# Moving layer 0's sums of h from GpSimd in the setup to VectorE in the first scores

## The chip, the cores and the metric
One core of a Trainium2 chip runs the whole program. Its engines are TensorE (PE, with its weight loads PEld), VectorE (DVE), ScalarE (ACT), GpSimd (POOL) and SyncE (SP, which here only issues DMAs). The metric is the time of one execution on the device in microseconds, the median of several runs.

## The reference
Two graph layers over N = 2708 nodes with D = 1024 features; `adj` is a sparse matrix of zeros and ones.
```python
# layer 0
h = jnp.maximum(_layernorm(x), 0.0)
f = h @ Wf + bf;  g = h @ Wg + bg
e = relu(f @ g.T)
attention = softmax(where(adj > 0, e, NEG), axis=1)
x = x + attention @ (h @ W + bW)
# layer 1
h = jnp.maximum(_layernorm(x), 0.0)
h1 = h @ W1
e = leaky_relu((h1 @ a1) + (h1 @ a2).T, 0.2)
x = x + relu(softmax(where(adj > 0, e, NEG), axis=1) @ h1)
```
All arithmetic is in float32.

## The kernel before, in words
**Panels and pairs.** The 2708 rows of the result are done in five panels of 512 to 576 columns (NP = 5). The contracted nodes lie in 20 full tiles of 128 rows, joined to ten pairs (NQ = 10), and two small tiles (MONO and TINY, together the unit LEFT).

**Seven products for eight.** Every large matrix product is done as a two-by-two block product with seven products, M1 to M7, in place of eight (a Strassen-Winograd scheme). It needs sums and differences of the blocks beforehand. For the product attention @ h the left blocks are rows of h: of a pair, ha = (ha0, ha1) and hb = (hb0, hb1), each half 128x512. The products use ha0 (M1), hb0 (M2), hb1 (M4), and four sums: s1 = ha1 + hb1 (M5), s2 = s1 - ha0 (M6), s3 = ha0 - ha1 (M7) and s4 = hb0 - s2 (M3). They are kept in device memory in `hg_d`, seven planes for each group of two pairs, and `aggregate` (from line 788) loads them as `hc`.

**Order of layer 0.** First a setup: the product M of the two weight matrices (`half_row_of_M`, from line 479), with the preparation of h in between. `make_pairs` (from line 336) puts the pieces of that preparation in a list `later`: for each pair, load x (`fetch`), layer norm (`normalize`: moments on VectorE, square root and scaling on ScalarE), `rows` (calls `pair_h`, line 297: the four sums above and the stores of the seven planes), `transposes` (TensorE, copied by ScalarE to the tiles hsT), dots with the vector vb (VectorE, lines 215 to 221, the result goes to `junk`), and `last` (line 373: sums of the transposed blocks on VectorE, stores to `hs_d`). Then `project_q(0)` (line 590) makes the right factor B of the first panel, and `scores(0)` (line 1055) multiplies the transposed rows, loaded as `As` from `hs_d` (line 1074), by B. For each pair q it also loads adjacency squares for q + 2 (`adj_i`, `adj_t`), turns them to masks, and has VectorE add the partial products. Then comes `project_q(1)`, with the softmax of panel 0 in between, then `aggregate(0, 0, ...)`, then the other panels and layer 1.

**What sets the order of the work.** A piece in `later` has a cost written by hand in microseconds. `behind(us)` (line 197) is called after groups of matmuls; it adds `us` to a credit, of at most twice `us`, and runs pieces while the credit is above zero. In `scores` the rate is 1.3 while pairs are still to be made, afterwards, for panel 0, 0.6; there are seven such units for a pair. `one()` (line 188) first issues the loads of the first `ahead[0]` pieces of the list, then runs the first piece. `ahead[0]` is 5 at the start and becomes 2 after `scores(0)` (line 1363).

**Queues and buffers.** All `load`s (line 137) go out on SP in program order; a load whose buffer isn't free holds up all that follow it. `store`s (line 141) go out on GpSimd's queue. Two sets of buffers matter: `slots`, 54 of 128x576, and `stream`, 12 of 128x1024. x, the score tiles, B, masks and scratch are slots; hsT, As, adj_i, hc, md and the tiles g1 and g2 of `pair_h` (two sums each, line 317) are streams. In `scores` VectorE's instructions keep their program order (`nc.hold`).

In layer 0 `pair_h` uses GpSimd (line 300) and always takes the way through g1 and g2, lines 317 to 327. In layer 1 it uses VectorE.

Of the kernel before, what the change touches and what calls it, by code (L numbers as in the profile page):

```python
# [19 lines left out]
W = 512  # L20
# [5 lines left out]
M1, M5, M6, M7, M3, M2, M4 = range(7)  # L26
# [31 lines left out]
def kernel(  # L58
# [230 lines left out]
    def left_h(l, hm, ht):  # L289

        for e in range(2):
            store(hgl_d[l][:, e, :W], hm[e])
            for d in range(NH):
                g = slice(B32 * d, B32 * (d + 1))
                store(hgl_d[l][g, e, W:], ht[e][g, d * P:(d + 1) * P])

    def pair_h(l, q, ha, hb):

        n = P
        on = nc.vector if l else nc.gpsimd  # L300
        if l and q >= NQ - F // 2:
            s1, s2, s3, s4 = (slot(f"g{i}")[:, :W] for i in range(4))
            i, j = group_of[q]
            for m, h in ((M1, ha[0]), (M2, hb[0]), (M4, hb[1])):
                store(hg_d[l][i][:n, m, j], h)
            on.tensor_tensor(s1, ha[1], hb[1], OP.add)
            on.tensor_tensor(s2, s1, ha[0], OP.subtract)
            for m, h in ((M5, s1), (M6, s2)):
                store(hg_d[l][i][:n, m, j], h)

            def rest():
                on.tensor_tensor(s4, hb[0], s2, OP.subtract)
                on.tensor_tensor(s3, ha[0], ha[1], OP.subtract)
                for m, h in ((M3, s4), (M7, s3)):
                    store(hg_d[l][i][:n, m, j], h)
            return rest
        g1, g2 = stream("g1", (P, 2, W)), stream("g2", (P, 2, W))
        s1, s2, s3, s4 = g1[:n, 0], g1[:n, 1], g2[:n, 0], g2[:n, 1]
        on.tensor_tensor(s1, ha[1], hb[1], OP.add)
        on.tensor_tensor(s2, s1, ha[0], OP.subtract)  # L320
        on.tensor_tensor(s3, ha[0], ha[1], OP.subtract)
        on.tensor_tensor(s4, hb[0], s2, OP.subtract)
        i, j = group_of[q]
        for m, h in ((M1, ha[0]), (M2, hb[0]), (M4, hb[1])):
            store(hg_d[l][i][:n, m, j], h)
        store(hg_d[l][i][:n, M5:M6 + 1, j], g1[:n])
        store(hg_d[l][i][:n, M7:M3 + 1, j], g2[:n])

    u = consts.tile([P, NC], FP, name="u")
    v = consts.tile([P, NC], FP, name="v")  # L330
    c0 = consts.tile([P, 1], FP, name="c0")
# [4 lines left out]
    def make_pairs():  # L336
        xs, hT = {}, {}

        def fetch(q):
            xs[q] = []  # L340
            for t in units[q]:
                xs[q].append(row_halves("x"))
                load_rows_of(t, xs[q][-1], x)

        def rows(q):
            left_h(0, *xs[q]) if q == LEFT else pair_h(0, q, *xs[q])

        def turned(q, k, e):
            t = units[q][k]
            ps = bank("h_ps", (P, NH, P))  # L350
            for c in range(NH):
                nc.tensor.transpose(ps[:, c, :], xs[q][k][e][:, c * P:(c + 1) * P], ident)
            for i, (s, n) in enumerate(pieces[0]):
                if s == t:
                    o = first_h[e].rearrange("p (c i) -> p c i", c=NH)[:, :, i * P:i * P + n]
                    nc.vector.tensor_copy(o, ps[:, :, :n])
            return ps

        def transposes(q):
            if q == LEFT:  # L360
                two = stream("hsl", (P, 2, NH, P))
                for e in range(2):
                    nc.scalar.copy(two[:, e], turned(q, 0, e))
                    nc.scalar.copy(tinyT[:, e], turned(q, 1, e)[:, :, :B32])
                store(hsl_d.rearrange("p e c j -> p (e c j)"), two.rearrange("p e c j -> p (e c j)"))
            else:
                ts = [stream("hsT", (P, 2, NH, P)) for _ in range(4)]
                hT[q] = ts, lambda i: ts[i // 2][:, i % 2]
                for k, e, i in ((0, 0, 0), (0, 1, 3), (1, 0, 7), (1, 1, 6)):
                    nc.scalar.copy(hT[q][1](i), turned(q, k, e))  # L370
            turned_tiles.update(units[q])

        def sums(q):
            if q == LEFT:
                return
            ts, i = hT.pop(q)
            at = {m: i(k) for k, m in enumerate(BY_SCORES)}
            add(at[M5], i(7), at[M4])
            sub(at[M6], at[M5], at[M1])
            sub(at[M7], at[M1], i(7))  # L380
            sub(at[M3], at[M2], at[M6])
            for g, t in enumerate(ts):
                store(hs_d[q][:, 2 * g:2 * g + 2].rearrange("p m c j -> p (m c j)"), t.rearrange("p m c j -> p (m c j)"))

        def dots(q, k):
            t = units[q][k]
            c = col_of[t]
            dot(r_[:, c:c + 1], xs[q][k], [vb[e][:, :W] for e in range(2)], c0)
            if t == MONO:
                nc.gpsimd.dma_start(r_[:NM, HALF:HALF + 1], r_[NM:, c:c + 1])  # L390

        def drop(q, what):
            seen.setdefault(q, set()).add(what)
            if len(seen[q]) == 3:
                xs.pop(q)

        def last(q):
            sums(q)
            drop(q, "sums")
            made.add(q)  # L400

        def bias(q, k):
            dots(q, k)
            drop(q, f"dots{k}")

        seen = {}
        def put_norms(q):
            put(2.1, lambda: normalize(xs[q][0]), lambda: fetch(q))
            put(2.1, lambda: normalize(xs[q][1]))

        put_rows = lambda q: put(0.5, lambda: rows(q))
        def put_dots(q):
            for k in range(2):
                put(1.6, lambda k=k: bias(q, k), ready=lambda: vb[0] is not None)

        todo = [0, 1, LEFT] + list(range(2, NQ))
        put_norms(todo[0])
        for i, q in enumerate(todo):
            if i + 1 < len(todo):
                put_norms(todo[i + 1])  # L420
            put_rows(q)
            put(0.5, lambda q=q: transposes(q), takes_psum=True)
            if i > 1:
                put_dots(q)
            put(2.7 if q != LEFT else 0.0, lambda q=q: last(q))
            if i == 1:
                put_dots(todo[0])
                put_dots(todo[1])

    def make_until(q):  # L430
        while min(q, NQ - 1) not in made:
# [342 lines left out]

    exps, LAG = [0], 2

    def exps_until(n):
        while exps[0] < n:
            one()
# [275 lines left out]
    def scores(p, B):  # L1055
# [46 lines left out]
        for q in range(NQ):  # L1102
            n = P
            make_until(q + 2)
            rate = 1.3 if NQ - 1 not in made else rates[p]
            if q + 2 <= LEFT:
                fetch(q + 2)
            sa, sb = slot("Sa"), slot("Sb")
            S[pairs[q][0]], S[pairs[q][1]] = sa, sb
            X, Y, Z = (bank(f"s{k}") for k in "xyz")  # L1110
            m1, t = slot("sm1"), slot("st")
            product(q, M1, X, True)
            for s in (lo, hi):
                add(m1[:n, s], X[:n, :h], rb[:n, s])
            if left_over:
                left_over()
            product(q, M6, Z, True)
            add(t[:n, lo], Z[:n, :h], m1[:n, hi])
            behind(rate, True)
            product(q, M5, Y, True)  # L1120
            add(t[:n, hi], Y[:n, :h], m1[:n, hi])
            if q + 1 <= LEFT:
                convert(q + 1)
            behind(rate, True)
            product(q, M2, X, False)
            add(sa[:n, lo], X[:n, :h], rb[:n, lo])
            if q + 1 <= LEFT:
                turn(q + 1, 0)
            behind(rate, True)
            product(q, M7, Z, False)  # L1130
            add(sb[:n, hi], Z[:n, :h], t[:n, hi])
            if q + 1 <= LEFT:
                turn(q + 1, 1)
            behind(rate, True)
            product(q, M3, Y, False)
            add(sa[:n, hi], Y[:n, :h], t[:n, lo])
            finish(q, sa, 0)
            behind(2 * rate, True)
            left_over = lambda q=q, sb=sb, Z=Z, m1=m1: last(q, sb, Z, m1)
# [220 lines left out]
    for p in range(NP):  # L1360
# [7 lines left out]
        else:  # L1368
# [2 lines left out]
            nc.hold = ()  # L1371
            scores_before()
        then = {M5: prepare_W} if p == 0 else {}
        if p == NP - 2:
            then[M2] = lambda: first_masks(NP - 1, 0)
            then[M6] = lambda: first_masks(NP - 1, 1)
            then[M7] = lambda: first_masks(NP - 1, 2)
# [132 lines left out]
```

## Time and profile before
| | |
|---|---|
| median of 4 runs | 3138.29 us (3137.76 to 3142.21) |
| the profiled execution | 3142.21 us, of which the span of the profile is 3140.1 us |
| DMA | 651.82 MB, mean 208 GB/s |
| setup | 0 to 152 us; `project_q(0)` 152 to 233; `scores(0)` 233 to 401 |
| GpSimd's sums in layer 0 (lines 319 to 322) | 40, each about 1.3 us, from 71 to 276 us |

How to read it: the page gives busy time, share of the span and count of instructions for each engine. A line of a timeline has start, duration (both us), engine, line, operation, out<-in and count. A line of waits has who waited, for whom, us in total, how often, and the longest. Almost all VectorE and ScalarE instructions show line 45, since a helper records them; they are told apart by their tiles. A table by stage lists, for each stretch, its length, busy us (and counts) of PE, PEld, DVE, ACT and POOL, then the granted clock of TensorE, the mean busy share of the 16 DMA engines, and GB/s.

### The profile page before, as it was taken

How to read it: one execution, taken by the hardware profiler on the slowest of the kernel's cores; microseconds unless marked ns; L12 is line 12 of the kernel's file. 1: busy time of each engine (PE TensorE's matmuls, PEld its weight loads, DVE VectorE, ACT ScalarE, POOL GpSimd, SP SyncE). 2: the span in 40 equal slices, each digit the busy share in tenths (PEclk: the TensorE clock that was granted, in tenths of full speed). 3: DMA queues.
4: the chain of work that ended last, by engine and by line, in shares of the span. 5: the costliest groups of instructions: out<-in, count | busy, mean ns of one | idle time of the engine just before them, and what ended most of it. 6: DMA issues, size and time to landing. Idle time of an engine off the chain costs nothing.

```text
span 3140.1 us, 36230 instructions
## 1 busy us (share of the span) xinstructions
PE 3052.8 (97%) x12712; PEld 2265.0 (72%) x12712; DVE 1826.9 (58%) x3730; ACT 447.2 (14%) x788; POOL 465.4 (15%) x668
## 2 busy tenths in 40 slices
PE   8988999999999999999999999998999999999998
PEld 4566777767877588876888885865757758678684
DVE  5867686286732687427872478659473571745612
ACT  3321020000200101000020002103031130311200
POOL 2643002210002110023000101021010020120202
PEclk9989999999999999999999999998999999999999
DMA  6889837878446796468955678596555565565655
GB/s 211 311 280 277 260 125 301 227 236 242 157 133 161 221 251 213 145 157 254 290 174 151 170 217 246 190 294 243 192 182 170 158 200 159 167 197 171 216 162 190
DMA packets 379109, 651.82 MB, mean 208 GB/s; under 512 B 170848, under 2 KB 211328, under 8 KB 378928
## 3 DMA queue, kind: packets, MB, share of 16 engines
q1 hardware_dynamic: 335920, 525.38, 54.6%
q0 software_dynamic: 43008, 124.13, 11.8%
q8 instruction: 101, 1.65, 0.2%
q14 instruction: 80, 0.66, 0.1%
HBM read 536.68 MB, written 112.67 MB: 207 GB/s over the span
## 4 chain that ended last, share of the span: by engine, by line
PE 85%; DMA 5%; DVE 4%; issue 3%; POOL 1%; SPq 1%; ACT 0%; POOLq 0%; DVEq 0%; ACTq 0%
PE gy L567 12%; PE gz L567 12%; PE gx L567 11%; PE sz L1077 7%; PE gv L567 5%; PE pz L969 5%; PE sx L1077 5%; PE sy L1077 4%; PE px L969 4%; PE py L969 4%; PE qz L567 3%; PE qy L567 2%; PE qx L567 2%; PE M_ps L483 2%; DMA maskl<-mk_d 1%
## 5 line engine op out<-in xcount | busy, mean ns | idle before, releaser
L1077 PE MATMUL sz<-B,As 128*128 128x288 f32 (+2 forms) x1200 | 293.0, 393 | 8.2 <-DVE st L45 7.5
L1077 PEld LDWEIGHTS sz<-B,As 128*128 128x128 f32 x1200 | 227.8, 191 | 58.4 <-DVE st L45 11.9
L873 POOL TENSOR_TENSOR gT<-gT,rr 128x2304 f32<-128x2304 f32 (+5 forms) x20 | 72.7, 3637 | 1102.9 <-DVE rr L45 1000.0
L1077 PE MATMUL sx<-B,As 128*128 128x288 f32 (+2 forms) x800 | 201.5, 395 | 13.0 <-DMA As<-hs_d 12.2
L1077 PE MATMUL sy<-B,As 128*128 128x288 f32 (+2 forms) x800 | 199.0, 392 | 0.0
L567 PE MATMUL gz<-P,hc 128*128 128x288 f32 (+2 forms) x800 | 186.0, 393 | 2.3 <-ACT gT L45 2.3
L567 PE MATMUL gz<-Sa,hc 128*128 128x288 f32 (+2 forms) x800 | 186.0, 393 | 2.3 <-ACT gT L45 2.3
L567 PE MATMUL gx<-P,hc 128*128 128x288 f32 (+2 forms) x800 | 186.8, 395 | 0.1
L1077 PEld LDWEIGHTS sx<-B,As 128*128 128x128 f32 x800 | 152.4, 191 | 44.8 <-DMA As<-hs_d 12.7
L567 PE MATMUL gy<-T,hc 128*128 128x288 f32 (+2 forms) x800 | 184.2, 391 | 0.0
L567 PEld LDWEIGHTS gx<-P,hc 128*128 128x128 f32 x800 | 153.5, 192 | 33.2 <-issue 1.9
L567 PEld LDWEIGHTS gz<-Sa,hc 128*128 128x128 f32 x800 | 151.2, 190 | 36.0 <-ACT gT L45 4.4
L567 PEld LDWEIGHTS gz<-P,hc 128*128 128x128 f32 x800 | 150.9, 190 | 35.7 <-ACT gT L45 4.5
L567 PEld LDWEIGHTS gy<-T,hc 128*128 128x128 f32 x800 | 152.0, 190 | 30.5
L1077 PEld LDWEIGHTS sy<-B,As 128*128 128x128 f32 x800 | 151.7, 190 | 30.6 <-DVE st L45 0.3
L969 PE MATMUL pz<-w,ps 128*128 128x512 f32 x320 | 142.1, 594 | 0.8 <-DVE pt L45 0.8
L969 PE MATMUL py<-w,ps 128*128 128x512 f32 x320 | 142.2, 593 | 0.0
L969 PE MATMUL px<-w,gT 128*128 128x512 f32 x320 | 141.8, 595 | 0.0
L143 POOL DMA_DIRECT2D out_dram<-x_res x180 | 89.2, 502 | 265.0 <-DVE x_res L45 242.3
L45 DVE TENSOR_TENSOR gT<-gy,u 128x288 f32<-128x288 f32 (+2 forms) x40 | 14.8, 431 | 183.5 <-PE gy L832 183.5
L45 DVE TENSOR_TENSOR u<-gz,m 128x288 f32<-128x288 f32 (+2 forms) x40 | 17.6, 439 | 171.2 <-PE gz L567 170.8
L143 POOL DMA_DIRECT2D mk_d<-mask x55 | 36.0, 655 | 543.2 <-DVE mask L45 520.0
(318 smaller groups left out, 5093.3 us busy)
## 6 DMA issues: line engine op xcount, KB each, us to landing
hc<-hg_d SPq DMA_DIRECT2D x350, 512.0 KB, 3.9
As<-hs_d SPq DMA_DIRECT2D x150, 512.0 KB, 5.2
w<-wt_d SPq DMA_DIRECT2D x96, 512.0 KB, 5.3
w<-in_L_gnn_W_dram SPq DMA_DIRECT2D x72, 512.0 KB, 4.2
md<-md_d SPq DMA_DIRECT2D x56, 512.0 KB, 4.5
adj_i<-in_adj_dram SPq DMA_DIRECT2D x200, 128.0 KB, 4.9
hs_d<-hsT POOLq DMA_DIRECT2D x40, 512.0 KB, 5.0
hg_d<-g POOLq DMA_DIRECT2D x36, 512.0 KB, 4.9
```

The costliest lines, as they stand in the source:

```text
L45: i = f(*a, **k)
L143: nc.gpsimd.dma_start(a, b)
L483: nc.tensor.matmul(ps, wfT[a][c // NH][:, c % NH, :], wgT[b][c], start=(c == 0), stop=(c == NC - 1))
L567: nc.tensor.matmul(ps[d], left(m, k, d), right(m, k), start=(start and k == 0), stop=(k == K - 1 and m not in more), skip_group_check=True)
L873: nc.gpsimd.tensor_tensor(of(e, s), of(e, s), by(s, k), OP.mult)
L969: nc.tensor.matmul(ps, left[i][m][:, k, :], w_[k], start=(start and k == 0), stop=(k == NH - 1), skip_group_check=True)
L1077: nc.tensor.matmul(ps[:n, :h], lefts[q][:, i % 2, c, :n], B[m][c // 2][:, c % 2, :h], start=(start and c == 0), stop=(c == NH - 1), skip_g ...
```

## The change
In layer 0 `rows` no longer calls `pair_h`. It stores ha0, ha1, hb0 and hb1 as they are, ha1 for now in the plane of M5. When all pieces of the preparation have been put in the list, `sums_h` puts two more pieces for each pair: the first has the four rows read back into four slots `hr` and makes s1 and s3 on VectorE in place, the second makes s2 and s4 and stores the four sums to their planes. Each has a written cost of 1.4. In `scores`, once all pairs are made, `ahead[0]` becomes 2. The first aggregation, after M1, runs whatever of these pieces is left.
```diff
     def pair_h(l, q, ha, hb):
...
-        on = nc.vector if l else nc.gpsimd
-        if l and q >= NQ - F // 2:
+        on = nc.vector
+        if q >= NQ - F // 2:
...
+    def rows_h(q, ha, hb):
+        i, j = group_of[q]
+        for m, h in ((M1, ha[0]), (M5, ha[1]), (M2, hb[0]), (M4, hb[1])):
+            store(hg_d[0][i][:, m, j], h)
+
+    summed = [0]
+
+    def sums_h():
+        def fetch(q, two):
+            i, j = group_of[q]
+            for m in (M1, M5, M2, M4):
+                two.append(slot("hr")[:, :W])
+                load(two[-1], hg_d[0][i][:, m, j])
+
+        def first(q, two):
+            a0, a1, b0, b1 = two
+            add(b1, a1, b1)
+            sub(a1, a0, a1)
+
+        def second(q, two):
+            a0, a1, b0, b1 = two
+            sub(a0, b1, a0)
+            sub(b0, b0, a0)
+            i, j = group_of[q]
+            for m, t in ((M5, b1), (M6, a0), (M7, a1), (M3, b0)):
+                store(hg_d[0][i][:, m, j], t)
+            summed[0] += 1
+        for q in range(NQ):
+            two = []
+            put(1.4, lambda q=q, two=two: first(q, two), lambda q=q, two=two: fetch(q, two))
+            put(1.4, lambda q=q, two=two: second(q, two))
...
-            left_h(0, *xs[q]) if q == LEFT else pair_h(0, q, *xs[q])
+            left_h(0, *xs[q]) if q == LEFT else rows_h(q, *xs[q])
...
+        sums_h()
...
+    def sums_until_all():
+        while summed[0] < NQ:
+            one()
...
             rate = 1.3 if NQ - 1 not in made else rates[p]
+            if NQ - 1 in made:
+                ahead[0] = 2
...
+        if p == 0:
+            then[M1] = sums_until_all
```

## The prediction
> **What bounds the kernel now.** I read the shares of the page first, then the windows of the first 609 us, then what TensorE waits for in them, then the timelines of the engines named there. The page says that TensorE is the bound of the whole:
> ```profile
> PE 3052.8 (97%) x12712; PEld 2265.0 (72%) x12712; DVE 1826.9 (58%) x3730; ACT 447.2 (14%) x788; POOL 465.4 (15%) x668
> ```
> So a change that adds no TensorE work can win only where TensorE stands still: 3140.1 - 3052.8 = 87 us in all. The table by stage (busy us of each engine, clock, DMA share, GB/s) shows how much of that lies in the part that is changed:
> ```profile
> 100.00:186.00 86.00, 71.39 (x229) 40.19 (x227) 74.73 (x143) 32.23 (x63) 58.94 (x85) 0.92 0.92 323
> 186.00:231.00 45.00, 44.61 (x181) 34.94 (x182) 23.95 (x53) 9.39 (x19) 19.15 (x24) 0.93 0.72 245
> 231.00:279.00 48.00, 35.19 (x156) 27.28 (x155) 34.73 (x81) 9.52 (x18) 21.51 (x27) 0.88 0.84 279
> 279.00:388.00 109.00, 109.00 (x456) 85.54 (x455) 72.53 (x155) 2.05 (x4) 5.99 (x11) 0.99 0.94 271
> ```
> Second number: TensorE; fourth: VectorE; sixth: GpSimd. In 100 to 186 TensorE is idle 14.6 us, VectorE nearly full, GpSimd busy 59. In 231 to 279 it is idle 12.8. In 279 to 388, the rest of the first scores, it never stops, but DMA is busy 0.94. The waits of TensorE name the three holes:
> ```profile
> PE sx L1077 <- DMA As<-hs_d: 12.2, 1, 12.2
> PE qx L567 <- ACT m L45: 8.9, 1, 8.9
> PE h_ps L352 <- ACT M L45: 5.2, 1, 5.2
> ```
> **Holes two and three are VectorE's, and it is GpSimd that holds it up.** ScalarE copies in order behind a square root that waits for VectorE's moments. The two timelines, side by side in time:
> ```profile
> 153.57 4.41 DVE L45 SCALAR_TENSOR_TENSOR junk<-x,vb 128x512 bf16<-128x512 f32 x1
> ...
> 158.52 0.74 DVE L45 SCALAR_TENSOR_TENSOR r<-part,c 128x1 f32<-128x1 f32 x1
> ```
> ```profile
> 153.71 1.28 POOL L319 TENSOR_TENSOR g<-x 128x512 f32<-128x512 f32 x1
> 154.95 1.26 POOL L321 TENSOR_TENSOR g<-x 128x512 f32<-128x512 f32 x1
> 156.17 1.25 POOL L320 TENSOR_TENSOR g<-g,x 128x512 f32<-128x512 f32 x1
> ```
> The same VectorE instruction takes 0.69 us elsewhere; here it ends only when three GpSimd sums have ended.
>
> **Hole one is a queue.** SP stands at adj_i from 252.3 until a stream buffer comes free, and the rows As of the third pair are behind it. What frees the buffer is the store of GpSimd's sums, as the chain of waits and SP's timeline show:
> ```profile
> 259.70 3.23 DMA hg_d<-g
> ```
> ```profile
> 262.98 3.71 SPq L139 DMA_DIRECT2D adj_i<-in_adj_dram  x4
> 266.74 2.57 SPq L139 DMA_DIRECT2D adj_t<-in_adj_dram  x4
> 269.41 9.70 SPq L139 DMA_DIRECT2D As<-hs_d  x4
> ```
> **What the Trainium skill says.** "SBUF — State Buffer", section Who interferes with whom: a VectorE instruction with two SBUF inputs contends with a GpSimd instruction that reads SBUF, and the loser is blocked for the whole instruction. The trace agrees, and more: 4.41 us spans three of them. "GPSIMD Engine Reference", section Elementwise: a two-input add is about twice as slow there as on VectorE. Here 1.27 us against 0.68 us (hsT sums of the same size), 1.9 times. "DMA: Bandwidth & Descriptors", section Issuing engines are not separate DMA queues: what SP and GpSimd issue runs on the same 16 DMA engines. That matters below; 0.82 of q1 and 0.12 of q0 add up to the 0.94 of 279 to 388.
>
> **The change, part by part.**
>
> (a) *Removed: 40 GpSimd sums* in the setup, 52.7 us of GpSimd (12.8 + 12.7 + 13.6 + 13.6). GpSimd is not the bound; the worth is what VectorE gets back. Excess over the normal duration of the same form, from 100 to 186: 110.4 us 1.2; 112.8 0.4; 115.1 1.2; 125.3 1.2; 135.4 3.7; 153.6 3.7; 158.5 0.5; 173.3 (hT, 4.48 against 1.35) 3.1; 177.9 0.9. Sum 16 us, against 14.6 us of TensorE idle. VectorE's 74.7 busy us become 59; with its hand-overs to ScalarE (the idle 11 us) that is 70 against TensorE's 71. So the two holes nearly close, and the ScalarE hand-overs (0.4 to 0.9 us each) become the late ones. I take 12 us; bounds 6 (the loads of x, whose buffers come late, end the waits instead) and 14.6 (all of it).
>
> (b) *Removed: two stream buffers a pair* (g1, g2) and three 256 KB stores a pair in the setup (7 become 4). For hole one the next buffer to come free is that of the hsT sums before, whose stores are issued by 249.3 us and land some 5 us later, at 254 instead of 263. From there, as now: 6.4 us to the As load, 5.6 us landing: 266, and TensorE, ready at 262.9, waits 3 us, not 12. I take 9; bounds 5 and 12.8.
>
> (c) *Added to VectorE: 40 sums* of 0.68 us, 27 us, in the first scores. By the queue's credit, seven steps of 0.6 a pair allow three pieces of 1.4 a pair, so they begin at the end of the third pair and are done in the ninth, six sums or 4.1 us a pair. VectorE is idle 109 - 72.5 = 36.5 us there; 8.7 of 13.6 us a pair becomes 12.8. Behind a late sum stand, in VectorE's written order, the adds that empty the accumulators; TensorE rewrites one two products (3.9 us) after it filled it, so a lag of about 3 us is free. I take 0; bounds 0 and 3. GpSimd's 40 new issues of 0.55 us lie in its idle time: 0. The first aggregation's check for unfinished sums finds none: 0.
>
> (d) *Added: 40 loads on SP and 40 stores on GpSimd's queue*, 256 KB each, 21.0 MB, nearly all from 279 to 388. There 29.6 MB move now. Of these 4.7 MB (nine md loads for the next stage) and of the new some 1.5 MB (last stores) can land later: 29.6 + 21.0 - 4.7 - 1.5 = 44.4 MB in 109 us, 407 GB/s. The highest long rate in the trace is 412 (500 to 525 us, large packets); with adj's packets under 512 B among them the busiest four-microsecond stretches give 375 to 380. At 380 the bytes take 117 us, 8 us too many. I take 8; bounds 0 (412 GB/s holds) and 25 (331 GB/s, the most that any of these stages reaches in 14 us, gives 134).
>
> (e) *SP's order.* Three pairs of rows (12 loads) are fetched in the third pair already, ahead of the adj and As loads of the fourth. At 0.47 us an issue (As: 1.90 us for four) that is 5.7 us; those As loads are now issued 8 us ahead of use and land in 5 to 7, so about 3 us are exposed. I take 3; bounds 0 and 8. From the fourth pair on SP's lead over TensorE is 10 to 17 us.
>
> The shorter look-ahead (2 for 5) takes hold only once all pairs are made and touches nothing but these sums. Nothing after the first aggregation changes: 0.
>
> **The sum.** -12 - 9 + 0 + 8 + 3 = -10 us. The profiled execution took 3142.21 us (span 3140.1), so it becomes 3132; the median of the four runs lies 3.9 lower, so **3128 us**. About 0.2% (6.3 us) is what a measurement of this kernel can tell from no change.
>
> **The rivals.**
>
> *Given back in the scores (22%).* The 21 us are won, but (d) costs 18 (44.4 MB at 350 GB/s take 127 us) and (e) 3: as before, 3138. For it: DMA at 0.94 already. Against it: share above 1 occurs[...], so the share overstates how full the engines are.
>
> *SP blocked by single buffers (27%): slower.* The rows read back take four slots a pair, and by the eighth pair some 43 of 54 slots are taken (18 score tiles, 14 of B, masks and scratch). A load of rows that waits on SP for the store of the sums two pieces before stands ahead of eight adj loads (4.5 us) and the As load (5 to 7 us landing). Once SP's lead is gone TensorE waits about 6 us a pair; over six pairs 36. 36 + 3 - 21 = 18 slower: 3156. It decides from a wait of SP longer than the 10 us lead, and needs four pairs of waits to end slower than before. For it: hole one is just such a wait. Against it: slots are short only from the seventh pair on, where it would cost 12 (then 3133, my forecast still).
>
> *Only the wins (14%).* (d) and (e) hidden by an earlier start of the loads: 3138 - 20 = 3118.
>
> *The change not doing what it says* can be excluded: all four sums of layer 0 have VectorE as engine.
>
> **How the numbers follow.** Forecast 37%, only wins 14%, given back 22%, blocked 27%. Forecast and only wins give 51% faster. Of given back, 21 fall within 0.2% and 1 beyond it on the slow side; with blocked that makes 28% slower. The faster cases' own range is 3115 to 3134. For 8 in 10 I reach from 3114 (27 won, of 14.6 + 12.8, less 3) to 3154, which holds most of the blocked case.
>
> **What would show it.** (a) right: the dot with vb stays at 0.69 us everywhere, ScalarE's wait for moments shrinks, TensorE's idle time in the setup falls below 5 us. (b) right: the 12.2 us wait for As is under 5. (d) or (e): TensorE waits for As in the pairs from the fourth on, with DMA near 400 GB/s. Blocked: SP waits on stores of the sums. Wrong altogether if the two holes stay with GpSimd silent: then x loads, not VectorE, bound the setup.

## The result, and the profile after
| | before | after |
|---|---|---|
| median | 3139.17 us (3135.99 to 3143.37, 61 runs) | 3144.10 us (3141.27 to 3148.44, 41 runs) |
| the profiled execution | 3142.21 us, span 3140.1 | 3142.71 us, span 3140.9 |
| ratio after / before | | 1.0016, 95% interval 1.0012 to 1.0021 |

The change makes the kernel 5 us slower; 10 us faster had been forecast. The two profiled executions lie at opposite ends of their kernels' spread (the one before 3.0 us above its median, the one after 1.4 below), so their spans differ by only 0.8 us. The traces can show where about 15 us were won and as many lost; they cannot place the last 4 of the 5.

TensorE's work is what it was (3052.8 us busy before), and so is its share:
```profile
PE 3052.6 (97%) x12712; PEld 2264.7 (72%) x12712; DVE 1825.4 (58%) x3770; ACT 447.7 (14%) x788; POOL 426.1 (14%) x658
```
What differs is where it stands still. First the table by stage of the kernel after (second number TensorE, fourth VectorE, sixth GpSimd, then clock, DMA share and GB/s), in the same stretches as before; the kernel is about 15 us further on from 186 us:
```profile
100.00:186.00 86.00, 86.00 (x305) 52.30 (x304) 60.67 (x146) 34.63 (x66) 31.84 (x59) 1.00 0.92 319
186.00:231.00 45.00, 45.00 (x206) 35.79 (x206) 33.26 (x75) 8.13 (x17) 7.54 (x14) 1.00 0.69 228
231.00:279.00 48.00, 33.73 (x141) 25.61 (x140) 32.03 (x75) 7.32 (x13) 8.64 (x16) 0.89 1.01 327
279.00:388.00 109.00, 94.73 (x367) 72.27 (x366) 79.52 (x155) 0.00 (x0) 23.84 (x44) 0.94 1.02 338
```
Three readings. In 100 to 186 TensorE now never stops: 14.6 us won. In 231 to 279 it is idle 48 - 33.7 = 14.3 us, where it was 12.8. In 279 to 388, where it did not stop before, it is idle 14.3 us, with the DMA share at 1.02 and 338 GB/s. Won and lost cancel. What TensorE waits for in the first 700 us says who does it:
```profile
PE sx L1116 <- DMA As<-hs_d: 21.3, 4, 8.4
...
PE sz L1116 <- DVE hsT L45: 4.6, 1, 4.6
...
PE sy L1116 <- DMA As<-hs_d: 2.6, 1, 2.6
```
The waits for ScalarE (8.9 and 5.2 us) are gone, and in place of one wait of 12.2 us for the rows As there are five, and one put down to VectorE's hsT sums. That last one is probably of the same kind: the product concerned (M7 of the third pair) also needed As rows issued at 252.9 us, after SP had waited 7.8 us for a stream buffer, which the stores of hsT sums held. The timeline of TensorE has the places (the third pair of scores begins at 241.8 us, the fourth at 272.6, the seventh at 319.8, the ninth at 360.7):
```profile
241.82 2.21 PE L1116 MATMUL sx<-B,As 128*128 128x288 f32 x8 [1.26 <-DMA As<-hs_d]
...
258.35 3.66 PE L1116 MATMUL sz<-B,As 128*128 128x288 f32 x8 [4.62 <-DVE hsT L45]
...
272.55 3.87 PE L1116 MATMUL sx<-B,As 128*128 128x288 f32 x8 [8.39 <-DMA As<-hs_d]
...
319.84 3.77 PE L1116 MATMUL sx<-B,As 128*128 128x288 f32 x8 [4.62 <-DMA As<-hs_d]
343.98 3.90 PE L1116 MATMUL sy<-B,As 128*128 128x288 f32 x8 [2.62 <-DMA As<-hs_d]
360.73 4.15 PE L1116 MATMUL sx<-B,As 128*128 128x288 f32 x8 [7.03 <-DMA As<-hs_d]
```
So (a) of the prediction held. The long wait at the start of the third pair, 12.2 us before, is 1.3; 4.6 us follow within that pair, 8.4 before the fourth, and 4.6 + 2.6 + 7.0 in the seventh to ninth. The reading back cost more than the prediction allowed. The theory for the experiments is that the bytes that are read and stored again in the first scores fill the DMA engines, so that As comes late. The rivals are SP's order (the rows stand ahead of As and adj), the twelve loads issued early, the ring of stream buffers, and VectorE's adds in its written order.

### The profile page after: what moved, and what is told of

Same layout as the page of the kernel before. It is cut to its first block, busy times and chain, and to the rows that moved or that the text cites. A ratio compares the mean times of both kernels' runs of the same rounds, so it can differ in the third digit from the quotient of the medians.

```text
span 3140.9 us, 36401 instructions
## 1 busy us (share of the span) xinstructions
PE 3052.6 (97%) x12712; PEld 2264.7 (72%) x12712; DVE 1825.4 (58%) x3770; ACT 447.7 (14%) x788; POOL 426.1 (14%) x658
## 4 chain that ended last, share of the span: by engine, by line
PE 80%; issue 10%; DVE 4%; DMA 4%; POOL 1%; SPq 0%; ACT 0%; POOLq 0%; DVEq 0%; ACTq 0%
PE gz L602 12%; PE gy L602 11%; PE gx L602 11%; PE pz L1008 5%; PE gv L602 5%; PE sz L1116 5%; PE px L1008 4%; PE py L1008 4%; PE sy L1116 3%; PE sx L1116 3%; PE M_ps L518 3%; PE qz L602 3%; PE qy L602 2%; PE qx L602 2%; PE po L979 1%
## 5 line engine op out<-in xcount | busy, mean ns | idle before, releaser
L1116 PE MATMUL sz<-B,As 128*128 128x288 f32 (+2 forms) x1200 | 293.7, 394 | 12.2 <-DVE st L45 6.9
L1116 PE MATMUL sx<-B,As 128*128 128x288 f32 (+2 forms) x800 | 205.1, 400 | 21.9 <-DMA As<-hs_d 21.3
L1008 PEld LDWEIGHTS pz<-w,ps 128*128 128x128 f32 x320 | 60.2, 190 | 77.1 <-issue 71.0
```

The lines of the kernel that those rows point to most:

```text
L1008: nc.tensor.matmul(ps, left[i][m][:, k, :], w_[k], start=(start and k == 0), stop=(k == NH - 1), skip_group_check=True)
L1116: nc.tensor.matmul(ps[:n, :h], lefts[q][:, i % 2, c, :n], B[m][c // 2][:, c % 2, :h], start=(start and c == 0), stop=(c == NH - 1), skip_g ...
```

## The experiments
Each is compared with the kernel before, whose median beside them was 3139.4 to 3140.2 us. Where a kernel leaves something out, the text says what.

**The sums left out.** The edit, in the kernel before:
```diff
+        for m, h in ((M1, ha[0]), (M2, hb[0]), (M4, hb[1]), (M5, ha[1]), (M6, ha[0]), (M7, ha[1]), (M3, hb[0])):
+            store(hg_d[0][i][:, m, j], h)
...
-            left_h(0, *xs[q]) if q == LEFT else pair_h(0, q, *xs[q])
+            left_h(0, *xs[q]) if q == LEFT else rows_h(q, *xs[q])
```


> The kernel before with layer 0's sums of h left out (the planes M5, M6, M7 and M3 get the rows themselves, so seven stores a pair remain, from the x tiles; the aggregation of layer 0 works on wrong data). It prices the GpSimd sums and their two stream buffers alone. Theory (the setup won about 15 us, and the first scores gave them back): 3139 - 15 for the setup, and the hole of 12 us in the first scores shrinks too if it was g1 and g2: 3112 to 3124. Rival (the hole in the first scores has little to do with GpSimd; the DMA traffic makes it): the setup's 15 only, and TensorE still idles 10 us or more between the second and the fourth pair: 3124.

Measured: 3110.22 us, ratio 0.9907 (0.9894 to 0.9921), more than either case. The two decisive stages of its table:
```profile
100.00:186.00 86.00, 86.00 (x312) 52.06 (x311) 63.31 (x153) 36.80 (x70) 42.40 (x79) 1.00 1.01 367
...
231.00:279.00 48.00, 43.95 (x190) 33.91 (x188) 39.07 (x92) 7.61 (x14) 9.77 (x19) 0.96 0.98 302
```
Idle 0 and 4.1 us: the setup's holes close and the one in the scores nearly does when GpSimd's sums go and nothing is read back. The sums on GpSimd with their two stream buffers cost 29 us, and that is the most that the change had to win.

**VectorE in the setup, nothing read back.**
```diff
-        on = nc.vector if l else nc.gpsimd
+        on = nc.vector
```


> The kernel before with one word changed: layer 0's sums by VectorE where they stand, in the setup, with g1 and g2 and no rows read back. It separates the engine from the place. VectorE's 74.7 busy us in 100 to 186 lose 16 and gain about 5 pairs of 2.7, 13.5: if VectorE's busy time were all that counts, the setup stays as it was, 3137 to 3141. If it is the single long blockings behind GpSimd (3.7 us each, ahead of the moments ScalarE waits for) that open the holes, it gains 5 to 10: 3129 to 3134. If the adds stand ahead of the moments in VectorE's order, it loses up to 10: 3149.

Measured: 3122.82 us, ratio 0.9944 (0.9932 to 0.9957): 17 us faster than before and 21 faster than the change. All three numbers that I gave were too high. In 100 to 186 VectorE is as busy as before, and yet TensorE's idle time falls from 14.6 to 3.1 us:
```profile
100.00:186.00 86.00, 82.88 (x287) 49.38 (x286) 72.91 (x172) 37.15 (x71) 37.15 (x65) 0.98 0.96 348
```
So it was not the sum of VectorE's busy time that hurt. That it was the blockings of up to 4.4 us ahead of the moments fits: the dot with vb takes at most 0.69 us here. It is argued from the trace, since in this run the buffers g1 and g2 may come free earlier too. What stays is a wait of 7.5 + 2.6 us for As in the scores.

**The rows over another queue.**
```diff
-                load(two[-1], hg_d[0][i][:, m, j])
+                tc.keep_in_program_order(nc.scalar.dma_start(two[-1], hg_d[0][i][:, m, j]))
```


> The changed kernel with the rows read back issued on ScalarE's queue, not SP's. Same bytes, same adds, same buffers; only the order on SP differs. Theory A (what was lost is SP's order: As and adj stand behind the rows): the waits for As from the third pair on, 8.4 + 4.6 + 2.6 + 7.0 us, fall below 8 in sum, 3125 to 3132. Theory B (DMA is full, 21 MB more in 109 us): the waits stay at 15 us or more, within 4 us of the changed kernel, 3140 to 3148.

Measured: 3151.44 us, ratio 1.0035 (1.0022 to 1.0048), slower than the change by 7. TensorE waits 31.6 + 4.7 us for As. SP no longer carries the rows, and its adj loads go out more slowly than ever. Two lines of SP's timeline, and one of ScalarE's for the rows that went out at the same time:
```profile
336.95 16.01 SPq L139 DMA_DIRECT2D adj_i<-in_adj_dram  x8
353.44 9.02 SPq L139 DMA_DIRECT2D adj_t<-in_adj_dram  x8
...
249.76 79.39 ACTq L45 DMA_DIRECT2D hr<-hg_d  x22
```
In the changed kernel the eight adj_i of this kind took 8.4 us. So SP's order is not what costs the time. That it even helped As against the rows is a likely reading; no run tests it by itself.

**One pair fetched early, not three.**
```diff
-            if NQ - 1 in made:
+            if q >= 2:
                 ahead[0] = 2
```


> The changed kernel with the short look-ahead from the third pair on, so that the rows of one pair, not of three, are fetched in the third pair. If the twelve loads ahead of the fourth pair's As make the 8.4 us wait, it falls below 3 and the kernel gains 5 to 8: 3136 to 3139. If that wait comes from the stream buffers (hsT stores) or from full DMA engines, it stays at 6 us or more: 3142 to 3146.

Measured: 3142.52 us, ratio 1.0010 (1.0003 to 1.0017). The wait before the fourth pair became 1.5 us, not 8.4:
```profile
263.78 2.21 PE L1116 MATMUL sx<-B,As 128*128 128x288 f32 x8 [1.53 <-DMA As<-hs_d]
...
279.00:388.00 109.00, 87.89 (x327) 66.43 (x326) 70.97 (x138) 0.00 (x0) 21.42 (x40) 0.91 1.02 327
```
But others grew: TensorE is idle 21.1 us in 279 to 388, where it was 14.3. The waits for As are 20.1 + 4.8 + 3.5 = 28.4 us in all, as in the changed kernel (21.3 + 4.6 + 2.6 = 28.5). They were moved, not removed.

**Half the bytes, the same number of issues.** Half the columns of the sums are left out; rows are stored in their place in the setup.
```diff
+        for m, h in ((M6, ha[0]), (M7, ha[1]), (M3, hb[0])):
+            store(hg_d[0][i][:, m, j, W // 2:], h[:, W // 2:])
...
-                two.append(slot("hr")[:, :W])
-                load(two[-1], hg_d[0][i][:, m, j])
+                two.append(slot("hr")[:, :W // 2])
+                load(two[-1], hg_d[0][i][:, m, j, :W // 2])
...
-                store(hg_d[0][i][:, m, j], t)
+                store(hg_d[0][i][:, m, j, :W // 2], t)
```


> The changed kernel with the same 40 loads, 40 stores and 40 adds, each over 256 of the 512 columns (the other half of the sums is left out; rows stand in the planes instead, stored in the setup). Number and order of the issues and the buffers are the changed kernel's; the bytes moved in the scores are halved, 10.5 MB. Theory (DMA is full of bytes): at the 338 GB/s that the changed kernel reached from 279 to 388 us, the stage's 29.6 + 10.5 - 6.2 = 34 MB need 100 of 109 us, so TensorE's waits for As drop from 28 us to under 12: 3118 to 3130. Rival (buffers and the number of issues on SP): they stay above 20 us, 3138 to 3145.

Measured: 3129.34 us, ratio 0.9963 (0.9950 to 0.9975): inside the theory's interval, 15 us faster than the change. The waits for As are 13.7 + 3.3 = 17 us, between the two cases' limits:
```profile
PE sx L1118 <- DMA As<-hs_d: 13.7, 3, 6.6
...
PE sz L1118 <- DMA As<-hs_d: 3.3, 1, 3.3
...
279.00:388.00 109.00, 103.00 (x441) 79.26 (x440) 75.19 (x166) 0.40 (x1) 22.98 (x43) 0.97 0.92 297
```
If the run with the sums left out stands for no bytes (3110.2), half (10.5 MB, 3129.3) and all (21 MB, 3144.1) make three points: 1.8 us for each of the first 10.5 MB and 1.4 for each of the others. So at this pace, begun in the third pair, there was no free room for the first megabytes either. Two runs further down show that there is some room later in the scores.

**No adds.**
```diff
-            add(b1, a1, b1)
-            sub(a1, a0, a1)
+            pass
...
-            sub(a0, b1, a0)
-            sub(b0, b0, a0)
```


> The changed kernel with its 40 VectorE adds in the scores left out; rows are read back and stored again as they are. Theory (27 us of adds are hidden on VectorE): 3141 to 3146, as the changed kernel. Rival (in VectorE's written order the late adds hold up TensorE): 10 us or more faster, 3134 or less.

Measured: 3149.97 us, ratio 1.0028 (1.0017 to 1.0039). The adds are not what makes the change slow; without them the kernel is even slower. A likely reason, not tested by itself: stores that need not wait for an add go out earlier and crowd As more (354 GB/s in 231 to 279 against 327, and a wait of 13.6 us at 278.6).

**Only the last two pairs read back, the others by VectorE in the setup.**
```diff
-    summed = [0]
+    summed, BACK = [0], NQ - 2
...
-        for q in range(NQ):
+        for q in range(BACK, NQ):
...
-            left_h(0, *xs[q]) if q == LEFT else rows_h(q, *xs[q])
+            left_h(0, *xs[q]) if q == LEFT else rows_h(q, *xs[q]) if q >= BACK else pair_h(0, q, *xs[q])
```


> Mixed: VectorE sums pairs 0 to 7 in the setup through g1 and g2, and only pairs 8 and 9 are read back in the scores (4.2 MB more there, not 21). Theory (little traffic fits into the 67 GB/s left free in the scores, and without g1 and g2 of the last two pairs the As rows of the third and fourth pair come earlier): the 10.7 us that TensorE waited between 248 and 274 us with VectorE in the setup shrink to about 4: 3113 to 3119. Rival (reading back costs whenever it is done): 3123 or more.

Measured: 3123.39 us, ratio 0.9944 (0.9931 to 0.9956), the rival's side by a hair, and not to be told from VectorE in the setup throughout. The 4.2 MB in the later pairs made no wait there (109.0 of 109 us busy in 279 to 388), but the hole before was not mended: 5.3 + 2.8 us for As.

**VectorE in the setup, sums in slots from pair 5 on.** `pair_h` takes its other branch, with four slots for the sums, for q >= 5 in layer 0.
```diff
-        on = nc.vector if l else nc.gpsimd
-        if l and q >= NQ - F // 2:
+        on = nc.vector
+        if q >= (NQ - F // 2 if l else NQ // 2):
```

> VectorE in the setup as in the run with one word changed, but from pair 5 on the sums lie in slots (four a pair) and not in the stream buffers g1 and g2. Theory (g1 and g2 in the ring of twelve are part of the hole in the first scores): the waits for As between 248 and 274 us go from 10.1 to under 5, 3115 to 3119. Rival (the hsT tiles alone fill the ring, or the x rows come later for want of slots): 3121 or more.

Measured: 3121.61 us, ratio 0.9939 (0.9926 to 0.9953). On the rival's side. The waits for As fell from 10.1 to 7.8 us, and 4.6 us of waiting for ScalarE came up in `project_q(0)`. Of the kernels here that compute all sums this is the fastest, level with the one-word edit.

**A ring of 13 stream buffers, with 52 slots**, in three kernels:
```diff
-    slots = ctx.enter_context(tc.tile_pool(name="slots", bufs=54))
-    strm = ctx.enter_context(tc.tile_pool(name="strm", bufs=12))
+    slots = ctx.enter_context(tc.tile_pool(name="slots", bufs=52))
+    strm = ctx.enter_context(tc.tile_pool(name="strm", bufs=13))
```


> The kernel before with 13 stream buffers and 52 slots, not 12 and 54. It asks whether the 12.2 us wait for As in the first scores is the ring of stream buffers. Theory: one more buffer lets the adj load go out earlier and the wait falls to 3 to 6 us, 3130 to 3135. Rival (SP waits for a store of GpSimd's sums whatever the ring): 3137 to 3141.

Measured: 3132.70 us, ratio 0.9979 (0.9972 to 0.9986): as the theory had it, the wait of 12.2 us is 7.1, though not as low as the 3 to 6 given. So the ring was part of that hole before. Another 2.7 us come from elsewhere: the first aggregation's wait for its operands is 1.6 us, not 4.3.

> The changed kernel with 13 stream buffers and 52 slots. Theory (the ring makes the 4.6 us wait in the third pair, and the bytes make the rest): 3137 to 3142. Rival A (the ring makes all the waits in the third and fourth pair): 3130 or less. Rival B (slots are short, so two slots less cost more than a stream buffer brings): 3146 or more.

Measured: 3139.38 us, ratio 1.0003 (0.9995 to 1.0011), in the theory's interval, but not for its reason: the waits are 20.7 + 3.6 + 3.2 us, hardly less, and the wait before the fourth pair rose from 8.4 to 10.2. Of the 5 us that this kernel is faster than the change, 2.3 lie in the first aggregation's wait (2.0 us, not 4.3). In the changed kernel the ring is not what keeps the hole open.

> VectorE in the setup, 13 stream buffers and 52 slots. With VectorE in the setup TensorE still waited 7.5 and 2.6 us for As, with SP waiting for hsT stores. Theory (ring): half of that goes, 3116 to 3119. Rival (VectorE makes the hsT sums late, and a buffer more doesn't help): 3121 to 3124.

Measured: 3125.99 us, ratio 0.9960 (0.9947 to 0.9973), slower than with 12 buffers and outside both cases. Waits of 3.1 and 7.1 us for As remain. Why was not looked into.

**Half the pace.** Everything is read back, added and stored, but the pieces' written cost is doubled, so that three pieces for two pairs of scores take the place of three for one; what is left over runs in `project_q(1)` and in the first aggregation, after M1.
```diff
-            put(1.4, lambda q=q, two=two: first(q, two), lambda q=q, two=two: fetch(q, two))
-            put(1.4, lambda q=q, two=two: second(q, two))
+            put(2.8, lambda q=q, two=two: first(q, two), lambda q=q, two=two: fetch(q, two))
+            put(2.8, lambda q=q, two=two: second(q, two))
```


> The changed kernel with written costs of 2.8, not 1.4, for the pieces of the sums: the same loads, adds and stores at half the pace, so that about half of the 21 MB move in the first scores and the rest in the next stage, where DMA is busy 0.4. Theory (bytes in the first scores): TensorE's waits for As fall from 28 us to 15 to 20, and what is left over costs little later: 3128 to 3136. Rival (the late half holds up the first aggregation, which needs M5 after M1): as much is lost there as won, 3140 to 3150, with TensorE waiting for hc.

Measured: 3127.93 us, ratio 0.9962 (0.9948 to 0.9976): 16 us faster than the change with the same loads, adds and stores. The table by stage of this kernel:
```profile
231.00:279.00 48.00, 33.96 (x142) 25.81 (x141) 32.08 (x76) 7.61 (x14) 8.64 (x16) 0.89 1.02 334
279.00:388.00 109.00, 109.00 (x474) 84.48 (x473) 84.25 (x165) 1.20 (x3) 17.89 (x33) 1.00 0.96 295
388.00:457.00 69.00, 67.04 (x278) 51.62 (x277) 61.81 (x113) 19.16 (x30) 4.34 (x8) 1.00 0.57 218
```
TensorE's 14.3 idle us in 279 to 388 are gone at 295 GB/s, and the next stage, where DMA was at 0.36 in the kernel before and 0.47 in the change, takes the rest for 2 us. Less was put off than the expectation has it: of the 80 transfers 16 (4.2 MB) were issued after 388 us, in the changed kernel none. The hole in 231 to 279 is as deep as in the change, 14.0 us; its twelve loads are issued as early as there.

**Half the pace and one pair early**, the two edits together, for that hole:

> The changed kernel at half pace (written costs of 2.8) and with the look-ahead of two pieces from the third pair on, so that the rows of one pair, not of three, are fetched in the third pair. If the twelve early loads make half of the hole of 14 us in the third and fourth pair, and at half pace nothing is lost later, it falls to about 7 and the kernel gains 5 to 8 on half pace alone: 3119 to 3123. If the early loads only moved the waits, 3126 to 3130.

Measured: 3129.19 us, ratio 0.9964 (0.9952 to 0.9977): the waits only moved. The hole is 7.4 us deep and 8.1 us are lost later:
```profile
231.00:279.00 48.00, 40.63 (x176) 31.12 (x175) 38.25 (x90) 7.61 (x14) 9.69 (x18) 0.96 1.00 322
279.00:388.00 109.00, 100.85 (x425) 77.17 (x424) 74.64 (x147) 0.40 (x1) 16.73 (x31) 0.97 0.94 292
```
This stage moved no more a second than at half pace alone (292 against 295 GB/s), and yet TensorE waited in it. So it is not the stage's mean rate alone that decides, but also how far the transfers have fallen behind when the stage begins; this was not taken further.

The last run has a stream buffer more besides:

> The run with half pace and one pair early, with 13 stream buffers and 52 slots besides. If what is left of the hole is the ring (SP waiting for the stores of the hsT sums), another 3 to 5 us go: 3115 to 3119. If slots are short instead, 3123 or more.

Measured: 3123.83 us, ratio 0.9945 (0.9932 to 0.9959), 5 us better than without the buffer. By the limits set, the rival's side; the ring is worth a few microseconds here, not the hole.

## Why the prediction was wrong
**The step that failed is (d), the rate at which the bytes move; next to it (e), the early loads.** The working let 44.4 MB pass in 279 to 388 at 380 GB/s, a rate taken from the busiest stretches of four microseconds, and came to 8 us. Measured are 14.3 us of TensorE idle there, in the seventh to ninth pairs, with DMA at 1.02 and 338 GB/s over the whole stage. The bytes that moved there are 36.9 MB, not 44.4: the kernel came to this stage further on than before, and twelve of the 40 loads had been issued ahead of it. The mechanism was right and inside its bounds, the rate was not.

What was taken for the rate of full engines is the rate of one mixture. In the changed kernel DMA moved 208 GB/s at a share of 1.19 from 325 to 330 us, when 2104 of 2246 packets were under 512 B, and 387 GB/s at 1.00 from 284 to 290, when 118 of 932 were. The kernel before had shown it too, in the fifth pair of its scores, again with the share and GB/s at the end:
```profile
307.00:320.00 13.00, 13.00 (x55) 10.22 (x54) 8.68 (x18) 0.00 (x0) 0.28 (x1) 1.00 1.09 245
```
The Trainium skill, "DMA: Bandwidth & Descriptors", section Where 436 GB/s comes from, gives about 358 GB/s as the limit of a core's share of HBM. The trace does not keep to one limit: the 412 GB/s of 500 to 525 us lie above it (one core runs here), and the first scores below it, at 338. The measured mixture decides.

That the bytes are the cause, and not the issues, the order on SP or the adds, rests on these runs: half the bytes with the same issues are 15 us faster; thinned out in time the same transfers leave no idle time in that stage and are 16 us faster; the rows on another queue, and no adds, make it slower. What is not explained is which wait a given amount of bytes brings: with half the pace and one pair early the same mean rate cost 8 us again.

The terms of the sum, by the waits in the two traces. SP's line for the As loads of the fourth pair, on which (e) turns:
```profile
267.35 2.84 SPq L139 DMA_DIRECT2D As<-hs_d  x4
```

- **(a), GpSimd's sums removed: right in kind, a little low.** 12 us were taken, 14.6 came, the upper bound. The dot with vb is at most 0.69 us throughout, as foretold.
- **(b), hole one: the mechanism was right, the size somewhat high.** 9 us were to come. The wait at the start of the third pair fell from 12.2 to 1.3 us, under the 5 that were named as its sign; but 4.6 us follow within that pair, where SP had waited for the next stream buffer. That leaves 6.3 us won. The idle time of 231 to 279 still rose by 1.5, because the early loads of (e) put a new wait there.
- **(c), the adds hidden: right** as far as is shown: without them the kernel is no faster.
- **(e), the twelve early loads: right in kind, mis-sized.** 3 us were taken, the wait before the fourth pair is 8.4, just beyond the bound of 8. Of SP's delay only the issue of twelve loads was priced, 5.7 us. In the trace SP also stood 7.8 us for a stream buffer, and the eight adj loads after it took 11.7 us to issue and not 6.3. So the As loads were issued at 267.4 us, 3 us after TensorE had become free for them, not 8 us ahead of use. Fetching one pair early made this wait 1.5 us, and the time was lost later, at full pace and at half; so (e) and (d) are not independent costs.
- **The sum.** By these waits -15.0 (with 0.4 us from 186 to 231) - 6.3 + 8.4 + 14.3 = 1.4 us, and the spans differ by 0.8. Forecast were -10: (d) misses by 6.3, (e) by 5.4, (b) by 2.7, and (a) is better by 3.
- **The rivals.** The one called given back was the right one: 21 us won, 18 lost by (d) at 350 GB/s and 3 by (e), 3138. Measured are 21.3 won, and 14.3 and 8.4 lost. It was held at 22%, and the result lies 6 us above it. SP blocked by single buffers for the rows is not what happened: SP's waits for stores of the sums are 6.8 us in all, and taking the rows off SP made it slower.
- **A term that was missing, but cancels.** In this trace each wait of 2.6 us or more is followed by slow matmuls: eight take 3.7 to 4.2 us and not 2.1, so such a hole costs some 2 us more than its idle time. The Trainium skill, "TensorE: Matmul & The Clock Gate", section What's actually happening, has half the clock rate after an idle stretch of some 3.4 us. The traces agree in kind and not in the length: eight matmuls took 3.9 us after a wait of 2.6 here, and 2.2 after a wait of 3.6 in the change with 13 stream buffers. TensorE's busy time in all is the same before and after, so the new holes seem to cost in this way what the old ones did. With the sums left out it is 3045.8 us for the same 12712 matmuls, 7 us less; the 29 us of that run are these 7 and some 22 of idle time.

What stays open: why the median is 5 us above the kernel before when the two profiled spans differ by 0.8; what keeps 5 us of waits for As in the third pair with VectorE in the setup and the sums in slots; and why 13 stream buffers make that kernel slower.

## What to carry to other kernels
Transfers that are moved into a busy stage must be priced at the rate that the stage sustains with its own mixture of packets, over its whole length; the best four microseconds of it are no measure. A high DMA share does not say how much room is left: the first scores, at 0.94 and 271 GB/s before, took 24 GB/s more at half pace without a wait, and 67 more with 14 us of waits. Keeping the rows in SBUF until they are summed would save the reading back; this was not tried. When two engines block each other, try to change the engine where the work stands before moving the work: here one word brought 17 us, and the change lost 5. A piece's pace can be worth as much as its place: the same transfers, thinned out, gained 16 us.

## What the hardware showed unexpectedly
- Moving the rows' loads to an idle queue made the kernel 7 us slower: 22 loads went out in 79 us beside SP's, and eight adj_i loads took 16.0 us to issue, not 8.4. One reading, not tested by itself, is that the order on one queue had protected the loads that matter.
- VectorE at the same busy time (72.9 against 74.7 of 86 us) left TensorE idle 3.1 us and not 14.6. A few blockings of up to 4.4 us ahead of what others wait for are the likely damage, not the load.
- At a DMA share above 1 the rate was anything from 208 to 412 GB/s: 208 (share 1.19) from 325 to 330 us, nearly all of it packets under 512 B, 338 (1.02) over the whole stage, and 412 (1.02) in 500 to 525 of the kernel before.
